# An attention layer with a second, four-token attention: next batch's token scores moved beside V on the Pool engine, the running maximum beside the V product, and the maximum spread by ScalarE

## The chip, the cores and the metric

The kernel runs on one core of one Trainium2 chip. The metric is device time in microseconds of one execution, as the median of several runs. Everything is float32. The engines that matter here are TensorE (PE in the profile), VectorE (DVE), ScalarE (ACT), GpSimd (POOL) and the DMA queue of SyncE (SP); each runs its own list of instructions in the order in which the program gives them.

## The reference

For each of 16 batches of 100 queries, ordinary attention over 718 context tokens is added to a second attention over 4 tokens, whose queries come out of a third, small attention. Shapes: x is 16x100x640, ctx is 16x722x384, eight heads of 80.

```python
enc, ca = ctx[:, :718], ctx[:, 718:]
hs = mha(x @ Wq, enc @ Wk, enc @ Wv)              # mha: softmax(q k^T / sqrt(80)) v, 8 heads
ca_q1 = einsum("btc,th->bch", ca, Wq_ca)[:, indices, :]   # indices: 100 of the 384 columns
ca_hs1 = mha(ca_q1, x, x)
ca_hs2 = mha(ca_hs1 @ Wq, ca @ Wk_ca, ca @ Wv_ca)
out = (hs + ca_hs2) @ Wout + b_out + x
```

## The kernel before

A loop over the 16 batches `b` does everything. On PE, DVE and POOL the order of instructions is the order in which the code is written (`tc.manual_schedule`); ScalarE's and the SP queue's order is made by a scheduler from the same program, and `tc.issue_after` places an instruction of ScalarE behind another one.

The 718 context tokens are cut into six chunks, worked on as three pairs (128, 128 and 103 rows each). For each pair, `scores(b, g, tiles)` multiplies keys and queries into four PSUM banks of the pool `ps4`, and ScalarE copies them into the tile `st` (L505). `larger` and L951 keep the running maximum `most` over all pairs on VectorE (two sums of SBUF tiles for a pair, written `ALU.max`).

V and the keys are formed by `Blocks`, a seven-product scheme over 2x2 blocks: `first_half` does four products into four PSUM banks and empties them into the destination (one ScalarE copy, three VectorE sums, L316 to L322), and `second_half` adds the other three into the same banks and empties them again (L327 to L333). The block sums that the scheme needs are made by POOL: `enc_sums` for each batch's context, `weight_sums` once. `values(b, i, enc)` gives V's three pairs `va`, `vb`, `vc`; `key_blocks` gives the next batch's keys `ka`, `kb`, and `last_keys` the last 128 rows of keys by plain products.

PSUM has eight banks: four of the pool `ps4` (scores, or a `room` for one `Blocks`), and four of `ps1`, taken in turn by all others: the banks of a `Blocks` without room, y, z, the transposed output, the output's product. A matmul that begins on a bank waits until whoever reads it has emptied it.

`Maximum` turns `most` into one maximum for each query: a 32x32 transposition `turned`, a reduction `quad`, four small reductions `side`, four `mx` (L547), a copy `spread` over 32 columns (L555) and a transposition back, `over`. They are steps of a generator; `top.go(n)` issues the next n. `subtract(i)` then takes `over` from pair i's scores (L930, 1600 columns), ScalarE makes the exponentials (L1066), and the product with V, `a_ps` (L1103), ends the batch on PE. VectorE divides by the sum (L1111, L1113) and adds the second attention `hs2` (L1119).

The second attention is the class `Second`: `products` (y on PE and g on VectorE), `copy` (y to SBUF by ScalarE), `scores1` (seven POOL instructions into `e1`, L624 and L631), `softmax1` (a `Maximum` of `e1` and a subtraction), `exponentials1` (ScalarE), `softmax2` (z on PE, divided by VectorE; it also issues the load of `vb` on POOL's queue, L668), `scores2`, `softmax3`, and `values2` (seven POOL instructions into `hs2`, L711 and L718). `now` is this batch's, `second` the next one's. `Last` is the output of the batch before: `load` (x by the SP queue, and POOL adds the bias), `transpose` (PE, then ScalarE into `hsT`), `project` (PE, then VectorE adds into `xn`, L787, and SP stores). Output rows are stored in tiles of 128, so `project` has 20 matmuls in most batches, none in batches 1, 5, 10 and 14, and 40 in batch 15. `keys(b + 2)` has POOL fill the matrix `m2` that `products` reads. In odd batches five products `queries` for the next two batches stand before `a_ps`.

In a middle batch PE's order before the change is: scores 0, `va` first half, scores 1, `va` second half, scores 2, transposition, `vb` and `vc` first halves, their second halves, `project`, y, z, `ka` and `kb` first halves, second halves, `last_keys`, queries (odd batches), `a_ps`. POOL's is: `values2`, `scores1` of the next batch, `keys`, then in the next batch `enc_sums`, the bias, and a wait for that batch's last subtraction.

Of the kernel before, what the change touches and what calls it, by code (L numbers as in the profile page):

```python
# [91 lines left out]
def kernel(  # L92
# [194 lines left out]
    class Blocks:  # L287
# [36 lines left out]
        def second_half(self):  # L324
            c11, c12, c21, c22 = self.to
            m = self.sum(0, ("12", "21"), ("31", "31"), last=True)
            self.copies.append(nc.scalar.copy(c11, m))  # L327
            m = self.sum(2, ("S4", "22"), ("31", "32"), last=True)
            nc.vector.tensor_tensor(c12, m, c21, ALU.add)  # L329
            m = self.sum(3, ("22", "T4"), ("32", "31"), last=True)  # L330
            nc.vector.tensor_tensor(c21, m, c21, ALU.add)
            m = self.sum(1, ("32", "32"), last=True)
            nc.vector.tensor_tensor(c22, m, c22, ALU.add)  # L333
# [12 lines left out]
    def weight_sums(to, raw):  # L346

        (w11, w12), (w21, w22) = raw
        for out, left, right, op in (
            (to[T1], w12, w11, ALU.subtract),  # L350
            (to[T2], w22, to[T1], ALU.subtract),
            (w12, w22, w12, ALU.subtract),
            (to[T4], w21, to[T2], ALU.subtract),
        ):
# [167 lines left out]
    class Maximum:  # L522


        def __init__(self, top, name):
            self.name = name
# [7 lines left out]
        def steps(self, top):  # L534
# [11 lines left out]
            for j in range(4):  # L546
                nc.vector.tensor_reduce(  # L547
                    mx[32 * j : 32 * j + 32, :],
# [6 lines left out]
            yield nc.vector.tensor_copy(spread, mx.unsqueeze(2).to_broadcast([P, NB, 32]))  # L555
# [15 lines left out]
    class Second:  # L571
# [75 lines left out]
        def softmax2(self):  # L647
# [18 lines left out]
            self.z = z  # L666
            self.vb = vb = vb_tile(f"vb_{b}")
# [239 lines left out]

    last = None
    engines = {mybir.EngineType.Pool, mybir.EngineType.PE, mybir.EngineType.DVE}
    ctx.enter_context(tc.manual_schedule(engines=engines))  # L910
    for b in range(B):
# [31 lines left out]
        if b == 0:  # L943
            now.softmax1()
        pair, copied = scores(b, 0, tiles)
        st.append(pair)
        if b == B - 1:
            now.softmax2()
        most = wide(f"most_{b}")
        top = Maximum(most, f"{b}")  # L950
# [5 lines left out]
        if b:  # L956
            va, vb, vc = (values(b, i, e_in) for i in range(NP))
            va.first_half()
        else:
            weight_sums(  # L960
                [wk2[:, j] for j in range(3)],
                [
                    [
                        wk_sb[:, c, : 4 * P].rearrange("p (i u n) -> p u i n", i=2, u=2)[:, u]
                        for u in range(2)
                    ]
                    for c in range(2)
                ],
            )
            nc.gpsimd.tensor_tensor(  # L970
                wk4, wk_sb[:, 1, 4 * P :], wk_sb[:, 0, 4 * P :], ALU.subtract
            )
            first_values(3, e_in, (act, act))
            now.exponentials1(copied)
# [7 lines left out]
        st.append(pair)  # L982
        larger(1)
# [4 lines left out]
        if b == 0:  # L988
# [6 lines left out]
        if 0 < b < B - 1:  # L995
            now.softmax1(2)
        if last:
            last.transpose()
        larger(2)
        if b == B - 2:  # L1000
            second.products()
            second.copy()
        if b == 0:
            first_values(5, e_in, (act, act), [1])
        elif b < B - 1:
            vb.first_half()
            now.softmax1(2)
            room = psum4(f"room_{b}")
            vc.first_half(room)
            now.softmax1()  # L1010
            top.go(2)
            vb.second_half()
            now.exponentials1(vb.copies[1])
            top.go(1)
            vc.second_half()
            top.go()
        else:
            vb.first_half()
            room = psum4(f"room_{b}")
            top.go(1)  # L1020
            vc.first_half(room)
            top.go(1)
            vb.second_half()
            top.go()
            subtract(0)
            vc.second_half()
            subtract(1, 2)
            last.project()


        if b + 1 < B:
            ka, kb = (key_blocks(b + 1, i, enc) for i in range(2))
            room = psum4(f"room1_{b}")
            if b:
                subtract(0)
                if last:
                    last.project()
                if b < B - 2:
                    second.products()
                now.softmax2()  # L1040
                ka.first_half(room)
                if b < B - 2:
                    with tc.issue_after(ka.copies[0].ins):
                        second.copy()
                now.scores2()
                subtract(1)
                now.softmax3()
                kb.first_half()
                less = subtract(2)
                ka.second_half()  # L1050
            else:
                second.products()
                ka.first_half(room)
                second.copy()
                kb.first_half()
                top.go()
                ka.second_half()
                subtract(0, 1, 2)
            kb.second_half()
            copies = ka.copies[1:] + kb.copies[1:] + last_keys(b + 1, enc)  # L1060
        else:
            copies = []
        for i, e in enumerate(st):
            after = copies[(0, 1, 1)[i] if b else 3] if copies else None
            with tc.issue_after(after.ins) if after else nullcontext():
                nc.scalar.activation(e, e, AF.Exp, scale=SCALE)  # L1066
        if b == B - 2:

            second.scores1()
            now.values2(less)  # L1070
            second.softmax1()
            second.exponentials1(copies[-1])
        elif 0 < b < B - 1:
            now.values2(less)
            second.scores1()
        elif b == 0:
            second.scores1()
            weight_sums(
                [wv2[:, j] for j in range(3)],
# [96 lines left out]
```

## Time and profile before

| | |
|---|---|
| median of 3 runs | 1057.51 us (1057.46 to 1057.79) |
| the profiled execution | 1057.47 us, its span 1055.8 us |
| mean granted clock of TensorE | 0.99 |
| busy: PE, DVE, POOL, ACT | 1012.4, 711.7, 505.1, 281.3 us |
| bytes moved | 59.92 MB, mean 57 GB/s |

The span runs from the first to the last instruction on the chip. A busy time is the sum of an engine's instructions; an engine can be waiting inside a stage and still have a high share over the whole. A row of the timeline gives start, duration, engine, line, operation, tiles written and read, shape, count, and in brackets the idle time before it and who ended it. A row of the waits gives who waited for whom, the total in microseconds, how often, and the longest. A row of the windows gives the busy time of each engine in a stretch and the granted clock (column PEclk).

### The profile page before, as it was taken

What the parts mean: (1) busy time and instruction counts of PE and PEld (TensorE: products, weight loads), DVE (VectorE), ACT (ScalarE), POOL (GpSimd) and SP (SyncE); (2) the same over time, 40 slices, a digit from 0 to 9 for tenths busy, and PEclk for the clock granted to TensorE, in tenths of its full rate; (3) what the DMA queues carried; (4) which work ended last, traced back from release to release, by engine and by line L of the source; (5) the groups of instructions that cost most, each with busy time, mean ns of one, the idle gap of its engine ahead of it and who ended that gap; (6) DMA issues with size and microseconds to landing.
All of it is one profiled execution on the core that took longest, in us unless ns stands there. A gap on an engine that the chain in (4) does not pass through costs nothing.

```text
span 1055.8 us, 25004 instructions
## 1 busy us (share of the span) xinstructions
PE 1012.4 (96%) x10945; PEld 745.3 (71%) x10945; DVE 711.7 (67%) x1277; ACT 281.3 (27%) x567; POOL 505.1 (48%) x439
## 2 busy tenths in 40 slices
PE   9997989999999999999999999998999999997997
PEld 6684758776686766867677676875768676685765
DVE  1348593867839686595946959377792877839884
ACT  1232221222322323223132221232222222322322
POOL 4639309056290644608365091723909047283660
PEclk9998999999999999999999999999999999999999
DMA  8631110211102020120201203011020201110100
GB/s 280 209 99 58 41 43 9 81 46 46 68 18 92 27 88 1 47 87 9 82 25 48 87 8 106 5 44 63 18 96 9 82 23 47 65 40 3 41 1 32
DMA packets 18014, 59.92 MB, mean 57 GB/s; under 512 B 2126, under 2 KB 8278, under 8 KB 14386
## 3 DMA queue, kind: packets, MB, share of 16 engines
q1 hardware_dynamic: 14658, 40.46, 11.7%
q0 software_dynamic: 2512, 16.72, 5.0%
q8 instruction: 86, 1.41, 0.6%
q10 hardware_dynamic: 736, 1.15, 0.3%
q14 instruction: 22, 0.18, 0.1%
HBM read 54.07 MB, written 4.26 MB: 55 GB/s over the span
## 4 chain that ended last, share of the span: by engine, by line
PE 63%; DVE 27%; issue 6%; ACT 3%; DMA 0%; DVEq 0%; ACTq 0%
PE a_ps L1103 11%; PE s_ps L495 11%; PE k_ps L299 9%; PE v_ps L299 8%; PE room L299 7%; PE kT_ps L437 7%; PE q_ps L412 6%; DVE mx L547 3%; DVE most L941 3%; DVE over L557 3%; ACT st L505 3%; PE v_ps L274 2%; DVE quad L539 2%; DVE turned L537 2%; DVE side L542 2%
## 5 line engine op out<-in xcount | busy, mean ns | idle before, releaser
L711 POOL TENSOR_TENSOR hs<-vb,p 100x640 f32<-100x640 f32 x64 | 82.9, 1304 | 456.4 <-DVE st L930 432.7
L299 PE MATMUL v_ps<-wv_sb,enc 128*128 128x320 f32 x480 | 154.7, 444 | 4.3 <-DVE v L320 1.7
L505 ACT COPY st<-s_ps 128x400 f32<-128x400 f32 (+1 forms) x192 | 80.5, 506 | 240.8 <-PE s_ps L495 240.6
L299 PEld LDWEIGHTS v_ps<-wv_sb,enc 128*128 128x128 f32 x480 | 85.8, 190 | 49.1 <-ACT hsT L764 8.5
L1103 PEld LDWEIGHTS a_ps<-v,st 128*64 128x64 f32 (+3 forms) x3072 | 111.1, 126 | 12.6 <-issue 12.5
L1103 PE MATMUL a_ps<-v,st 128*64 128x81 f32 (+3 forms) x3072 | 113.8, 236 | 6.3 <-DVE kT L329 6.3
L624 POOL TENSOR_TENSOR e<-ca,g 100x800 f32<-100x800 f32 x64 | 103.1, 1621 | 27.2 <-issue 21.6
L941 DVE TENSOR_TENSOR most<-most,st 128x800 f32<-128x800 f32 (+1 forms) x64 | 82.7, 1292 | 46.5 <-ACT st L505 45.4
L1111 DVE RECIPROCAL rs<-a_ps 100x4 f32<-100x4 f32 x32 | 5.8, 182 | 158.8 <-PE a_ps L1103 158.8
L495 PEld LDWEIGHTS s_ps<-qp,kT 32*128 32x128 f32 (+1 forms) x3072 | 92.3, 179 | 15.3 <-issue 7.7
L631 POOL TENSOR_TENSOR e<-e,e 100x800 f32<-100x800 f32 x48 | 99.3, 2068 | 3.8
L495 PE MATMUL s_ps<-qp,kT 32*128 32x100 f32 (+1 forms) x3072 | 100.4, 267 | 0.0
L299 PE MATMUL k_ps<-enc,wk_sb 128*128 128x359 f32 x240 | 85.0, 476 | 10.0 <-DVE xn L787 7.3
L930 DVE TENSOR_TENSOR st<-st,over 128x1600 f32<-128x1600 f32 (+1 forms) x48 | 91.5, 1910 | 0.5
L299 PE MATMUL room<-enc,wk_sb 128*128 128x359 f32 x240 | 86.2, 482 | 0.0
L299 PE MATMUL room<-wv_sb,enc 128*103 128x320 f32 x240 | 75.9, 434 | 3.1 <-DVE v L320 3.1
L718 POOL TENSOR_TENSOR hs<-hs,hs 100x640 f32<-100x640 f32 x48 | 75.8, 1579 | 3.8
L1066 ACT ACTIVATE st<-st 128x1600 f32<-128x1600 f32 (+1 forms) x48 | 72.4, 1536 | 11.0 <-DVE st L930 10.9
L299 PEld LDWEIGHTS k_ps<-enc,wk_sb 128*128 128x128 f32 x240 | 45.3, 192 | 41.5 <-DVE xn L787 13.0
L777 PE MATMUL o_ps<-wout_sb,hsT 128*128 128x320 f32 (+2 forms) x260 | 71.9, 432 | 0.0
L412 PEld LDWEIGHTS q_ps<-xT,wq_sb 128*128 128x128 f32 x400 | 67.9, 190 | 2.1 <-issue 0.5
L437 PE MATMUL kT_ps<-enc,wk_sb 128*128 128x359 f32 x210 | 68.7, 465 | 0.5 <-ACT kT L440 0.5
(133 smaller groups left out, 1578.5 us busy)
## 6 DMA issues: line engine op xcount, KB each, us to landing
enc<-in_enct SPq DMA_DIRECT2D x15, 1077.0 KB
vb<-va_d POOLq DMA_DIRECT2D x16, 1000.0 KB, 5.9
xT<-in_xt SPq DMA_DIRECT2D x8, 500.0 KB
xn<-in_x SPq DMA_DIRECT2D x11, 320.0 KB
out<-xn SPq DMA_DIRECT2D x11, 320.0 KB
ca<-in_cas SPq DMA_DIRECT2D x16, 156.2 KB
wout_sb<-in_wqt SPq DMA_DIRECT2D x1, 1600.0 KB
wq<-in_wq SPq DMA_DIRECT2D x5, 320.0 KB
```

Source lines behind the costliest of these rows:

```text
L299: nc.tensor.matmul(bank[: left.shape[1], : right.shape[1]], left, right, start=(first and i == 0), stop=(last and i == len(products) - 1), ...
L412: nc.tensor.matmul(q_ps[:, : 2 * S].rearrange("p (j s) -> p j s", j=2), wq_sb[:, c, n * P : (n + 1) * P], xT[:, :, c, :], start=(c == 0), ...
L437: nc.tensor.matmul(k_ps[:, :KH], w, a, start=(c == 0), stop=(c == CC - 1))
L495: nc.tensor.matmul(s_ps[r][:n, 256 * a + lo : 256 * a + hi], kT[rows, c, k : k + n], rhs, start=(a == 0 and c == 0), stop=(c == HC - 1), s ...
L505: copied = nc.scalar.copy(st[:, :, 2 * r * S : 2 * (r + 1) * S], s_ps[r][:n].rearrange("p (a q) -> p a q", a=2)[:, :, : 2 * S],)
L624: first = nc.gpsimd.tensor_tensor(to, self.ca[:, t, :].unsqueeze(1).to_broadcast([S, NH, S]), g[:, :, t].unsqueeze(2).to_broadcast([S, NH, ...
L631: nc.gpsimd.tensor_tensor(e, e, to, ALU.add)
L711: first = nc.gpsimd.tensor_tensor(to, vb[:S, t, :].rearrange("p (h d) -> p h d", h=NH), p2[:, :, t].unsqueeze(2).to_broadcast([S, NH, D]), ...
L718: nc.gpsimd.tensor_tensor(sums, sums, to, ALU.add)
L930: less = nc.vector.tensor_tensor(st[i], st[i], top.over[:n].unsqueeze(1).to_broadcast([n, 2, ROWS]), ALU.subtract,)
L941: nc.vector.tensor_tensor(most[:n], most[:n], st[i][:, u], ALU.max)
L1103: nc.tensor.matmul(a_v[lo:hi, h % 4], st[i // 2][:, i % 2, h * S + lo : h * S + hi], block(i, h // 4)[:, h % 4], start=(i == 0), stop=(i = ...
```

## The change

- In middle batches `now.softmax2` (z) and `second.products` and `copy` (y) come right behind the third scores, ahead of V's second and third pair; they stood behind `project`.
- `second.scores1` (the next batch's `e1`) is issued on POOL behind y, beside V; it stood behind `values2`. In batch 0 it waits for the last subtraction (`less`).
- The maximum's first steps are issued ahead of and between the first halves of `vb` and `vc`; `vb` uses the room in `ps4`, `vc` the banks of `ps1`. The first subtraction stands before `vc`'s second half.
- `Maximum` with `behind` makes two `mx` reductions in place of four, and ScalarE makes `spread` in two copies of 64 rows; `vb.second_half` puts its ScalarE copy behind them.
- `softmax1` of the next batch moves from V's stage of its own batch to the key stage of the batch before (batch 1's own stays in batch 1, behind `va`'s first half), and `exponentials1` goes behind the first ScalarE copy of `va`.
- In `second_half`, bank 1 is used and emptied second, where it was last.
- `vb`'s load is issued at the start of the batch (`now.load`).
- Batch 0: three of the four sums of Wv's blocks are made early on POOL, the fourth behind `values2`; y comes before the last plain V product; all exponentials stand behind the last key copy.
- Which ScalarE copy each exponential follows is changed: `kb`'s first, `ka`'s second, `kb`'s second.

```diff
-        def second_half(self):
+        def second_half(self, behind=None):
             m = self.sum(0, ("12", "21"), ("31", "31"), last=True)
-            self.copies.append(nc.scalar.copy(c11, m))
+            with tc.issue_after(behind.ins) if behind else nullcontext():
+                self.copies.append(nc.scalar.copy(c11, m))
+            m = self.sum(1, ("32", "32"), last=True)
+            nc.vector.tensor_tensor(c22, m, c22, ALU.add)
             m = self.sum(2, ("S4", "22"), ("31", "32"), last=True)
             nc.vector.tensor_tensor(c12, m, c21, ALU.add)
             m = self.sum(3, ("22", "T4"), ("32", "31"), last=True)
             nc.vector.tensor_tensor(c21, m, c21, ALU.add)
-            m = self.sum(1, ("32", "32"), last=True)
-            nc.vector.tensor_tensor(c22, m, c22, ALU.add)
...
     def steps(self, top):
-            for j in range(4):
+            self.scalar = scalar = self.behind is not None
+            rows = 64 if scalar else 32
+            for lo in range(0, 64 if scalar else P, 32):
                 nc.vector.tensor_reduce(
-                    mx[32 * j : 32 * j + 32, :],
+                    mx[lo : lo + 32, :],
...
-            yield nc.vector.tensor_copy(spread, mx.unsqueeze(2).to_broadcast([P, NB, 32]))
+            if scalar:
+                for lo in range(0, P, rows):
+                    with tc.issue_after(self.behind().ins):
+                        self.spreading = nc.scalar.copy(
+                            spread[lo : lo + rows],
+                            mx[:rows].unsqueeze(2).to_broadcast([rows, NB, 32]),
+                        )
+            else:
+                nc.vector.tensor_copy(spread, mx.unsqueeze(2).to_broadcast([P, NB, 32]))
+            yield
...
         if b == 0:
             now.softmax1()
+        now.load()
         pair, copied = scores(b, 0, tiles)
...
+            if b == 1:
+                now.softmax1()
...
+            weight_sums([wv2[:, j] for j in range(3)], wv_raw, range(3))
             first_values(3, e_in, (act, act))
-            now.exponentials1(copied)
...
         pair, copied = scores(b, 1, tiles)
+        if 0 < b < B - 1:
+            now.exponentials1(copied if b == 1 else va.copies[0])
         larger(1)
...
         pair, copied = scores(b, 2, tiles)
         if 0 < b < B - 1:
-            now.softmax1(2)
-        if last:
-            last.transpose()
+            now.softmax2()
         larger(2)
-        if b == 0:
-            first_values(5, e_in, (act, act), [1])
-        elif b < B - 1:
-            vb.first_half()
-            now.softmax1(2)
-            room = psum4(f"room_{b}")
-            vc.first_half(room)
-            now.softmax1()
-            top.go(2)
-            vb.second_half()
-            now.exponentials1(vb.copies[1])
-            top.go(1)
-            vc.second_half()
-            top.go()
...
+        if b == 0:
+            second.products()
+            second.copy()
+            first_values(5, e_in, (act, act), [1])
+            weight_sums([wv2[:, j] for j in range(3)], wv_raw, [3])
+            ka, kb = (key_blocks(b + 1, i, enc) for i in range(2))
+            top = Maximum(most, f"{b}", lambda: kb.copies[0])
+            top.go(1)
+            ka.first_half(psum4(f"room1_{b}"))
+            top.go(1)
+            kb.first_half()
+            top.go(1)
+            top.go()
+            less = subtract(0, 1, 2)
+            ka.second_half()
+            kb.second_half()
+        else:
+            top = Maximum(most, f"{b}", lambda: vc.copies[0])
+            if b < B - 1:
+                second.products()
+                second.copy()
+            last.transpose()
+            if b < B - 1:
+                second.scores1()
+            top.go(2)
+            vb.first_half(psum4(f"room_{b}"))
+            top.go(1)
+            vc.first_half()
+            top.go()
+            vb.second_half(top.spreading)
+            if b < B - 1:
+                now.scores2()
+            subtract(0)
+            if b == B - 1:
+                subtract(1)
+            vc.second_half()
+            if b < B - 1:
+                now.softmax3()
+                ka, kb = (key_blocks(b + 1, i, enc) for i in range(2))
+                last.project()
+                ka.first_half(psum4(f"room1_{b}"))
+                subtract(1)
+                kb.first_half()
+                less = subtract(2)
+                if b < B - 1:
+                    second.softmax1(2)
+                ka.second_half()
+                second.softmax1(1)
+                kb.second_half()
+            else:
+                subtract(2)
+                last.project()
+        if b + 1 < B:
+            copies = [kb.copies[0], ka.copies[1], kb.copies[1]]
+            final = last_keys(b + 1, enc)
...
+        if b == 0:
+            second.scores1(less)
+        elif b < B - 1:
+            now.values2(less)
+            second.softmax1()
+        if b == B - 2:
+            second.exponentials1(final[-1])
```

## The prediction

> **What bounds the kernel now.** I read the page's engine totals first, then the Tensor engine's waits, then one batch's timeline on every engine, then the granted clock around the gaps.
>
> ```profile
> PE 1012.4 (96%) x10945; PEld 745.3 (71%) x10945; DVE 711.7 (67%) x1277; ACT 281.3 (27%) x567; POOL 505.1 (48%) x439
> PE 63%; DVE 27%; issue 6%; ACT 3%; DMA 0%; DVEq 0%; ACTq 0%
> ...
> PE room L299 <- DVE v L329: 7.6, 4, 1.9
> PE k_ps L299 <- DVE xn L787: 7.3, 10, 1.0
> PE a_ps L1103 <- DVE kT L329: 6.3, 1, 6.3
> PE room L299 <- DVE v L320: 3.1, 6, 0.5
> PE k_ps L299 <- DVE z L663: 2.7, 1, 2.7
> ```
>
> PE is the bound: it is almost never idle, and nearly all its waits are for VectorE to empty a PSUM bank. So only PE's lost time can be won. I took it from PE's timeline: wherever two matmul starts lie further apart than is usual for that shape, the excess is lost. Batch by batch (0 to 15): 7.15, 4.91, 0.94, 3.47, 0.93, 6.09, 0.92, 2.09, 0.94, 2.09, 4.88, 2.09, 0.93, 2.07, 7.84, 2.50; together 49.8 us. The rest is matmul work that the change keeps, so no outcome is below about 1008. Batches 1, 5, 10 and 14 stand out: no output tile is ready there, `project` (20 matmuls, 5.4 us) is missing, and that was VectorE's time to catch up:
>
> ```profile
> 713.38 0.74 PE L652 MATMUL z_ps<-y,e 100*32 100x33 f32 x64 [0.66 <-DVE v L329]
> 716.85 2.26 PE L299 MATMUL room<-enc,wk 128*128 128x359 f32 x4 [1.93 <-DVE v L329]
> ...
> 717.40:720.70 3.30, 3.30 (x6) 1.92 (x6) 3.23 (x4) 0.00 (x0) 0.00 (x0) 0.50 0.01 4
> ```
>
> The last row is the window view (PEclk is the column with 0.50): after the gap PE runs at half clock for 3.4 us, worth 1.7 us.
>
> ```profile
> 626.19 3.46 DVE L941 TENSOR_TENSOR most<-most,st 128x800 f32<-128x800 f32 x2 [2.13 <-ACT st L505]
> 652.61 1.82 DVE L930 TENSOR_TENSOR st<-st,over 128x1600 f32<-128x1600 f32 x1
> 92.79 8.48 DVE L930 TENSOR_TENSOR st<-st,over 128x1600 f32<-128x1600 f32 x3
> 664.46 2.50 POOL L711 TENSOR_TENSOR hs<-vb,p 100x640 f32<-100x640 f32 x2 [26.79 <-DVE st L930]
> 643.93 0.87 ACT L645 ACTIVATE e<-e 100x800 f32<-100x800 f32 x1 [6.41 <-DVE e L641]
> 659.17 1.54 ACT L1066 ACTIVATE st<-st 128x1600 f32<-128x1600 f32 x1
> ```
>
> VectorE's sums of two SBUF tiles are slow while Pool works: 3.46 for two `larger` against 2.02 in batch 0, and 2.83 for a subtraction against 1.82. Its sums from PSUM are not (0.49 either way). Pool idles 26.8 us in mid-batch.
>
> **The change in a batch with project (2-4, 6-9, 11-13).** I count from the first score matmul, with starts and durations of batch 9 (616.64).
> PE: third scores end at 13.99; z 0.68, y 1.06 and the transpose 0.48 now follow (they were elsewhere, so no work is added), then V's second pair: first halves from 16.2 and 18.45, second halves 20.6 and 24.4, project 28.15 (second bank 30.84).
> VectorE: `larger(1)` now meets an idle Pool, since the next tokens' scores no longer run into this batch: 2.0 instead of 3.46. z's two operations (0.62) fit before 15.85, when ScalarE has copied the third scores. Then `larger(2)` to 17.8, g to 18.0, transposition and reduction to 19.9, V sums 21.5, side and two mx (0.74 + 0.65; two of 0.32 are dropped) 22.9, V sums 24.45.
> ScalarE spreads: a row for a copy of 64x800 is missing. Below: the exponential of 100x800, 0.87; above: that of 1600 elements, 1.54. I take 0.87, the same count of elements. Two end at 24.65, so VectorE's spread copy (0.99) is gone and `over` hardly waits, ending 25.6. Behind it in the queue stand V sums (27.0) and `scores2`'s three (0.96), so the subtraction starts at 27.96.
> Pool: g releases 12.2 us of products (four of 1.54, three of 1.88, gaps) from 18.1 to 30.3, across that subtraction. Row: 2.83 (mean of batch 0's three), ending 30.8. The next V sum frees project's second bank at 31.35 against 30.84: 0.5 lost. The Trainium skill (SBUF — State Buffer, "SBUF: two separate sides") says that the port pair is locked for a whole instruction and the loser blocks: up to 1.88 + 1.82 = 3.70, a loss of 1.4. The row is of this very instruction, so I keep 0.5; by the rule the total would be some 11 us worse.
> Key stage: softmax3 and the xn sums end at 34.7; `subtract(1)` 38.45, `subtract(2)` 41.8 with Pool idle. The next maximum's halves (1.9 and 2.1) now stand ahead of the key sums; the sum that frees last_keys' second bank ends at 47.65, wanted at 48.8: hidden by 1.1. Its spread, over and e1 (3 to 4 us) lie beside a_ps, where VectorE idled (158.8 us in front of L1111 in all). Without that cover they would hold the rs sums. The xn wait of 1.0 (ten times) goes, as three key banks no longer need it early.
> Lost: 0.5 in place of 0.92-2.09 (3.47 in batch 3): 16.5 becomes 5.0, **-11.6**.
>
> **Batches 5, 10, 14.** The V pair ends at 28.15 and keys follow at once. Key sums wait 0.1. Then VectorE, with two half maxima ahead of the sums, frees last_keys' second bank at 45.4, wanted at 43.4: a stall of 2.0, a new one in place of L329's. The clock: the gaps of 1.9 (in batches 1, 5 and 10) and 2.7 (batch 14) were each followed by half clock, those of 1.2 (batch 3) and 1.8 (batch 14) were not. The skill (TensorE: Matmul & The Clock Gate, the table of two states) throttles after an idle window of about 3.4 us, which would cost nothing here; the rows say 1.7. Mine lies at the edge, so I take half, 0.85. Sum 2.95 each: 18.8 becomes 8.9, **-9.9** (by the rule -12.5).
>
> **Batch 1** does the next maximum in its V stage (7.0 us after V's first sums); ScalarE's exponential stands in front of its copies of the third scores: z waits to 15.8 (1.8), y for a V sum 0.4. Then as above 0.3 and 2.3, clock 0.85: 5.65 for 4.91, **+0.75**.
> **Batch 0**: with `less` Pool no longer works beside the three subtractions (5.3 for 8.48) and the key sums end near 97.6, not 101.9; but the exponentials stand behind the last key copy (96.0) and end at 100.5, and PE, idle from 95.4, draws the half clock again. I take **-1.5**, between 0 and -4.
> **Batch 15**: `larger(2)` still collides with Pool's values2 (3.98), and now the transposition and reduction precede V's sums: they end about 22.9, wanted at 20.7, a stall of 2.15; project's second bank waits 1.45; 1.0 of old stalls goes: **+2.6**.
>
> **Moved and costless**: vb's DMA goes ahead of enc_sums on Pool's queue (0.58 a batch; landing 5.9 us after issue, due over 20 us later); in batch 0 it waits there for va_d, whose landing no row shows: between 0 and some 7 us (the longest vb landing), ahead of sums that PE wants only at 77.7 and which ended at 65.0. wv sums (3 x 0.86) move ahead of values2(0), which waits for p2 until 76.7: hidden. On SP the ca and enc loads stand ahead of the out stores and xn loads; the same count, and xn is due a batch later: nothing. Pool's m2 and enc_sums keep their place behind values2; without values2's early start they would reach `larger(1)` again (1.4 a batch). Swapping wk's third and fourth sum and freeing V's bank 1 first (c22 before c12) costs nothing and lets y start at 14.7, its bank being free at 12.0.
>
> Sum: -11.6 - 9.9 + 0.75 - 1.5 + 2.6 = -19.7. The profiled execution took 1057.47 (span 1055.8 and 1.67 around it), 0.04 below the median 1057.51. **1038.**
>
> **Rivals.**
> 1. *The spread decides (slower).* `over` waits in VectorE's strict order, and behind it everything to project's second bank has no slack. At 1.54 each the two copies cost 1.3 more in each of 14 batches (18), and the gaps of 1, 5, 10, 14 surely draw the clock (3.4): 1038 + 21.6 = 1060. It outweighs the gain from about 1.45 a copy. For: nothing covers it. Against: 0.87 for 800 elements. 14%.
> 2. *Pool's collision is worse.* Subtractions of 3.5 (the longest L930 here), V sums and last_keys late by 0.7 to 0.9 in 13 batches: 1048 to 1050. For: Pool's span reaches past 30; against: one subtraction of three is hit. 20%.
> 3. *The stall only moves*: the key stage's half maxima are late by 1 to 2 us in all batches too, eating the 1.1 of slack: about 1055 to 1060. 10%, split evenly over the three signs near zero.
> 4. *No clock drops, no collision*: 1028 to 1031. 10%.
> Main case 46%, its own range 1031 to 1045.
>
> **How the numbers follow.** Faster: 46 + 20 + 10 + a third of rival 3 (3) = 79, less 1 for what I overlooked: 0.78. Same (within 0.2%, 2.1 us, about what a measurement can tell): 0.05. Slower: rival 1 and the last third: 0.17. The range runs from 1026 (no collision, no clock, batch 0 at its best) to 1058, leaving out most of rival 1 and little below.
>
> **What would show it.** In the changed profile: no L941 pair above 2.1 in mid-kernel batches; ScalarE's spread rows of about 0.87; subtract(0) at 2.5 to 3 and the other two at 1.82; PE waits on o_ps for VectorE of about 0.5, on kT_ps in batches 1, 5, 10, 14 of about 2, on batch 15's V of about 2; the wait on xn gone; four half-clock stretches or fewer in the loop. I am wrong if spread rows exceed 1.4, if kT_ps waits in project batches, or if odd batches stay at 68.3.

## The result, and the profile after

The changed kernel takes 1021.03 us (median of 4 runs, 1020.68 to 1021.13), beside 1057.57 for the kernel before on the same chip: ratio 0.9654, 95% interval 0.9637 to 0.967. That is 36.5 us less, where 19.5 less was predicted; the direction was right, and the time lies below the predicted range. The profiled execution has a span of 1019.0.

The engine totals, the granted clock in 40 slices, and the shares of the chain that ended last:

```profile
PE 996.0 (98%) x10945; PEld 745.6 (73%) x10945; DVE 670.9 (66%) x1229; ACT 312.3 (31%) x599; POOL 503.5 (49%) x439
...
PEclk9999999999999999999999999999999999999999
...
PE 89%; DVE 6%; DMA 2%; SPq 1%; ACT 1%; issue 1%; DVEq 0%; ACTq 0%
```

VectorE's share of the chain fell from 27% to 6% and PE's rose from 63% to 89%: PE now almost only follows itself. VectorE lost 41 us of busy time: about 1.6 a batch for the spread copy and two mx reductions, 14 in `larger` (82.7 to 68.7), 5 in the subtractions; against these, a small subtraction of the second attention (L704) takes 0.6 instead of 0.2 in 13 batches. ScalarE gained 31, most of it the spreads (1.72 in each of the 16 batches).

PE's waits for other engines (total, how many, longest):

```profile
PE kT_ps L441 <- DVE kT L331: 5.5, 4, 1.7
PE a_ps L1110 <- DVE kT L331: 2.2, 1, 2.2
...
PE room L299 <- DVE v L318: 1.7, 1, 1.7
...
PE z_ps L668 <- ACT v L329: 1.6, 1, 1.6
...
PE o_ps L796 <- DVE v L331: 1.0, 1, 1.0
```

Each of these waits is in a batch without `project` or in batch 0 or 15. In the ten batches that have it, there is none left. (Below, a stall is the distance between two matmul starts less the usual one for that shape; it comes out about 0.15 longer than the idle time in a row's brackets. The 1.7 on kT_ps is a stall of 1.88.) That shows in project itself, in batch 9 (first score matmul at 596.62):

```profile
624.63 5.55 PE L796 MATMUL o_ps<-wout_sb,hsT 128*128 128x320 f32 x20
...
624.42 0.59 DVE L704 TENSOR_TENSOR e<-s,mx 100x32 f32<-100x32 f32 x1
624.93 1.81 DVE L959 TENSOR_TENSOR st<-st,over 128x1600 f32<-128x1600 f32 x1
626.67 0.48 DVE L331 TENSOR_TENSOR v<-v_ps,v 103x320 f32<-103x320 f32 x1
...
623.43 1.54 POOL L640 TENSOR_TENSOR e<-ca,g 100x800 f32<-100x800 f32 x1
625.04 3.45 POOL L647 TENSOR_TENSOR e<-e,e 100x800 f32<-100x800 f32 x1
...
619.51 1.72 ACT L565 COPY spread<-mx 64x800 f32<-64x800 f32 x2 [3.41 <-DVE mx L554]
```

The first row holds all 20 matmuls of project in one run without a gap. VectorE and Pool do meet, but the subtraction takes its 1.81; Pool's sum is the one held up (3.45; undisturbed 1.88). The two spread copies take 1.72, 0.86 each; 0.87 was predicted.

The batch periods (first score matmul to the next batch's first) say where the time came from:

| batches | before, us | after, us | predicted gain | measured gain |
|---|---|---|---|---|
| with project (2-4, 6-9, 11-13) | 58.6, odd ones 68.3 to 69.8 | 57.3, odd ones 65.75 | 11.6 | 21.0 |
| 5, 10, 14 | 67.25, 57.56, 60.25 | 62.36, 53.90, 53.90 | 9.9 | 14.9 |
| 1 | 66.0 | 64.57 | -0.75 | 1.4 |
| 0 | 49.46 | 47.84 | 1.5 | 1.6 |
| 15 | 57.58 | 60.02 | -2.6 | -2.4 |

The start before the loop gave another 0.3. So nearly the whole miss is in the first three lines.

### The profile page after: what moved, and what is told of

Read it like the earlier page. It is cut to its first block, busy times and chain, and to the rows that moved or that the text cites. A ratio compares the mean times of both kernels' runs of the same rounds, so it can differ in the third digit from the quotient of the medians.

```text
span 1019.0 us, 24988 instructions
## 1 busy us (share of the span) xinstructions
PE 996.0 (98%) x10945; PEld 745.6 (73%) x10945; DVE 670.9 (66%) x1229; ACT 312.3 (31%) x599; POOL 503.5 (49%) x439
## 4 chain that ended last, share of the span: by engine, by line
PE 89%; DVE 6%; DMA 2%; SPq 1%; ACT 1%; issue 1%; DVEq 0%; ACTq 0%
PE room L299 17%; PE v_ps L299 17%; PE s_ps L499 12%; PE a_ps L1110 11%; PE k_ps L299 8%; PE q_ps L416 7%; PE o_ps L796 7%; PE kT_ps L441 7%; PE y_ps L605 2%; DMA kT<-in_wkt 1%; DVE st L959 1%; PE z_ps L668 1%; SPq L207 1%; PE hst_ps L774 1%; PE v_ps L274 1%
## 5 line engine op out<-in xcount | busy, mean ns | idle before, releaser
L640 POOL TENSOR_TENSOR e<-ca,g 100x800 f32<-100x800 f32 x64 | 97.8, 1539 | 292.7 <-ACT v L316 265.1
L730 POOL TENSOR_TENSOR hs<-vb,p 100x640 f32<-100x640 f32 x64 | 82.7, 1303 | 151.9 <-DVE st L959 129.4
L299 PE MATMUL v_ps<-wv_sb,enc 128*128 128x320 f32 (+1 forms) x480 | 151.9, 439 | 0.0
L299 PEld LDWEIGHTS v_ps<-wv_sb,enc 128*128 128x128 f32 (+1 forms) x480 | 83.7, 179 | 44.6 <-issue 6.7
L647 POOL TENSOR_TENSOR e<-e,e 100x800 f32<-100x800 f32 x48 | 112.1, 2336 | 3.8
L970 DVE TENSOR_TENSOR most<-most,st 128x800 f32<-128x800 f32 (+1 forms) x64 | 68.7, 1073 | 45.4 <-ACT st L509 44.3
L959 DVE TENSOR_TENSOR st<-st,over 128x1600 f32<-128x1600 f32 (+1 forms) x48 | 86.8, 1814 | 0.0
L299 PE MATMUL room<-enc,wk_sb 128*128 128x359 f32 x240 | 82.2, 464 | 0.0
L299 PE MATMUL k_ps<-enc,wk_sb 128*128 128x359 f32 x240 | 82.2, 464 | 0.0
L299 PE MATMUL room<-wv_sb,enc 128*128 128x320 f32 x240 | 75.8, 438 | 1.7 <-DVE v L318 1.7
L441 PE MATMUL kT_ps<-enc,wk_sb 128*128 128x359 f32 x210 | 69.8, 467 | 6.0 <-DVE kT L331 5.5
L416 PE MATMUL q_ps<-xT,wq_sb 128*128 128x200 f32 x400 | 69.1, 333 | 0.0
```

The source lines that it names most:

```text
L299: nc.tensor.matmul(bank[: left.shape[1], : right.shape[1]], left, right, start=(first and i == 0), stop=(last and i == len(products) - 1), ...
L416: nc.tensor.matmul(q_ps[:, : 2 * S].rearrange("p (j s) -> p j s", j=2), wq_sb[:, c, n * P : (n + 1) * P], xT[:, :, c, :], start=(c == 0), ...
L441: nc.tensor.matmul(k_ps[:, :KH], w, a, start=(c == 0), stop=(c == CC - 1))
L640: first = nc.gpsimd.tensor_tensor(to, self.ca[:, t, :].unsqueeze(1).to_broadcast([S, NH, S]), g[:, :, t].unsqueeze(2).to_broadcast([S, NH, ...
L647: nc.gpsimd.tensor_tensor(e, e, to, ALU.add)
L730: first = nc.gpsimd.tensor_tensor(to, vb[:S, t, :].rearrange("p (h d) -> p h d", h=NH), p2[:, :, t].unsqueeze(2).to_broadcast([S, NH, D]), ...
```

## The experiments

Eleven kernels ran, each beside the kernel before on the same chip.

**1. ScalarE's spread undone in the changed kernel.**

```
- top = Maximum(most, f"{b}", lambda: vc.copies[0])
+ top = Maximum(most, f"{b}")
- vb.second_half(top.spreading)
+ vb.second_half()
```

> The changed kernel with one part undone: in batches 1 to 15 VectorE spreads the maximum itself again (four mx reductions in place of two, its own copy of 128x800), and V's second pair no longer waits for ScalarE's spread. Theory: PE's waits vanish in the batches with project because VectorE's chain from the V sums to project's second bank lost 1.6 us (0.64 for two mx and 0.97 for the spread copy), so that the first subtraction is done when PE asks for that bank. Put back, the subtraction starts near 626.5 instead of 624.93 in batch 9, behind Pool's last product sum, and the bank comes 1.5 to 2 us too late: ten batches by about 1.8, and little elsewhere, so about 1021 + 18 = 1039 (1036 to 1042), with waits on o_ps for VectorE of 1.5 to 2 us. Rival: the spread was a small part and VectorE had the time anyway (the gain comes from e1's maximum having left the V stage): 1021 to 1025, no wait on o_ps over 0.5.

Measured: 1053.99 us, ratio to before 0.9964 (0.9949 to 0.9978). Of 36.5 us only 3.8 are left (2.3 to 5.4 by the interval). Each batch with project takes 1.95 longer (59.23 and 67.69). The waits of PE, and batch 9 (which starts at 614.89 here):

```profile
PE o_ps L796 <- DVE v L331: 19.3, 11, 2.6
...
PE k_ps L299 <- DVE v L331: 4.1, 3, 1.4
...
644.18 1.06 DVE L704 TENSOR_TENSOR e<-s,mx 100x32 f32<-100x32 f32 x1
645.16 1.81 DVE L959 TENSOR_TENSOR st<-st,over 128x1600 f32<-128x1600 f32 x1
646.90 0.48 DVE L331 TENSOR_TENSOR v<-v_ps,v 103x320 f32<-103x320 f32 x1
...
643.31 1.88 POOL L647 TENSOR_TENSOR e<-e,e 100x800 f32<-100x800 f32 x1
...
642.90 2.86 PE L796 MATMUL o_ps<-wout_sb,hsT 128*128 128x320 f32 x10
647.43 2.96 PE L796 MATMUL o_ps<-wout_sb,hsT 128*128 128x320 f32 x10 [1.67 <-DVE v L331]
```

Project breaks in two. The subtraction starts 30.27 after the batch's start instead of 28.31, and 1.67 of PE's idle time follows, with a late start of the matmul behind it. The delay has two parts. The small L704 starts 1.49 later (29.29 for 27.80), which is about the two mx reductions and the copy (1.6 us); then it waits 0.47 longer for Pool's sum (1.06 for 0.59). PE loses the whole of it, 1.95 per batch: the chain from V to project has no slack. Ten batches give 19.4. Batches 5 and 10 lose 3.6 each, 14 loses 2.0 (a k_ps wait of 1.4 in each, and half clock in the first two), batch 1 loses 2.0, batch 15 loses 1.5, and 1.3 lie ahead of the loop, where this edit changes nothing. The theory's mechanism held, but it was sized only for the project batches: 1036 to 1042 was too low.

**2. The spread alone, in the kernel before** (batches 1 to 14; two mx reductions and VectorE's copy go, two ScalarE copies come; nothing else moves). In this kernel's code the two stand behind ScalarE's copy of the second half of `vc`, not of the first half as the expectation says; in batch 9 they start as soon as mx is there.

> The kernel before with one part of the change alone: in batches 1 to 14 ScalarE spreads the keys' maximum in two copies of 64x800 behind V's last first-half copy, and VectorE drops two mx reductions and its spread copy. Nothing else is moved. Theory: VectorE reaches the first subtraction about 1.5 us earlier, which takes away the waits behind it (k_ps for xn, 0.7 to 1.0 in ten batches, and some small ones) but not those of the V stage ahead of it (the room waits of 1.9 us in batches 1, 5, 10 and 14, y and z): 1057.5 - 7 to 11 = 1046 to 1051. Rival: the spread is the whole gain, as undoing it in the changed kernel cost 33 us: 1022 to 1030. Second rival: nothing, since the ends of the V stage are set elsewhere: 1056 to 1058.

Measured: 1038.03, ratio 0.9812 (0.9796 to 0.9829): 19.3 us gained, twice what I expected, though not the rival's 30. Even project batches fall from 58.6 to 57.84, odd ones to 66.5 to 67.3; these ten give 12.8 of it. In the loop, three of the four half-clock stretches of the kernel before (batches 1, 10 and 14) are gone as well, which I had not counted. With experiment 1 this makes a square of gains over the kernel before, each against its own runs on the same chip:

| | rest as before | rest changed |
|---|---|---|
| VectorE spreads | 0 | 3.8 |
| ScalarE spreads | 19.3 | 36.5 |

(It is not quite square: the second row's left kernel spreads by ScalarE in batches 1 to 14 alone, the first row's right one still does in batch 0.) Alone the spread gives 19.3 and the rest 3.8; together they give 36.5. The rest brings 17.2 only once the spread is there. The two don't add up because both work on one chain: moving e1's maximum and z takes waits away from the V stage, but without the spread VectorE reaches project's second bank too late all the same.

**3. The next tokens' scores again at the batch's end** (batches 1 to 13: Pool behind `values2`, VectorE's maximum in the next V stage).

```
-            if b == 1:
+            if b < B - 1:
                 now.softmax1()
...
-            now.exponentials1(copied if b == 1 else va.copies[0])
+            now.exponentials1(copied)
...
-            if b < B - 1:
+            if b == B - 2:
                 second.scores1()
...
-                if b < B - 1:
+                if b == B - 2:
                     second.softmax1(2)
                 ka.second_half()
-                second.softmax1(1)
+                if b == B - 2:
+                    second.softmax1(1)
...
             now.values2(less)
-            second.softmax1()
+            if b == B - 2:
+                second.softmax1()
+            else:
+                second.scores1()
```

> The changed kernel with the move of the next tokens' scores undone for batches 1 to 13: Pool computes them again behind values2, at the batch's end, and VectorE takes their whole maximum in the next batch's V stage, as the changed kernel does only in batch 1; ScalarE's spread and the early z and y stay. Theory: each of batches 2 to 13 then looks like batch 1 of the changed kernel, which loses 1.9 in front of z, 0.5 in front of y and 1.7 by half clock: 2.4 to 4.1 us each, plus a little for larger beside Pool, and less the 1.9 of the kT_ps stall in batches 5 and 10: 1021 + 30 to 45 = 1051 to 1066. Rival: ScalarE's spread was all of it, and the move of the scores is worth little: 1021 to 1030.

Measured: 1068.72, ratio 1.0107 (1.0092 to 1.0122): 1% slower than the kernel before, and a little above what I expected. Batches 2 to 13 lose 48.2 together against the changed kernel; ten half-clock stretches fall into them, where the changed kernel has none. PE's waits, and batch 9 of this kernel:

```profile
PE z_ps L668 <- ACT v L329: 36.0, 14, 5.2
...
636.84 1.54 DVE L657 TENSOR_TENSOR e<-e,over 100x800 f32<-100x800 f32 x1
638.29 2.01 DVE L970 TENSOR_TENSOR most<-most,st 128x800 f32<-128x800 f32 x2
...
638.47 0.87 ACT L661 ACTIVATE e<-e 100x800 f32<-100x800 f32 x1 [6.07 <-DVE e L657]
...
639.79 0.74 PE L668 MATMUL z_ps<-y,e 100*32 100x33 f32 x64 [2.86 <-ACT v L329]
```

The subtraction of e1's maximum ends at 638.4, and e1's exponential (638.47, 0.87) must follow; so z is late. The releaser named is ScalarE's V copy, which stands behind that exponential in ScalarE's queue. With e1's maximum in the V stage, early z and y cost more than ScalarE's spread brings: the parts of this change need one another. Early z and y, the exchanged banks of `vb` and `vc` and the earlier load of `vb` were not undone one by one.

**4. Pool idle when the first subtraction runs.** From batch 2's tokens on, Pool makes only the first of the four products of the next tokens' scores and leaves the other three and their sums out, so the second attention of this kernel is incomplete.

```
-            for t in range(T):
+            for t in range(T if b < 2 else 1):
```

> The changed kernel, but of the four products of the next tokens' scores Pool computes only the first (from batch 2's tokens on), so that Pool is idle when the first subtraction runs. Theory: VectorE pays nothing for Pool's work beside it, because its subtraction begins first and Pool's sum is the one held up (3.45 instead of 1.88 us): 1021 within 1 us, the first subtraction 1.81 as before, the small e2 sum back from 0.59 to 0.19. Rival: Pool's work beside V still costs VectorE some tenths that PE sees as small restarts: 1014 to 1018.

Measured: 1018.97, ratio 0.9634 (0.9619 to 0.9648), 2.1 less than the changed kernel. The project batches take 57.29 and 65.75, exactly as with Pool busy, so the collision costs them nothing. What is gained is 0.4 in each of batches 1, 5, 10 and 14, by the small sum:

```profile
623.21 0.19 DVE L704 TENSOR_TENSOR e<-s,mx 100x32 f32<-100x32 f32 x1
623.32 1.82 DVE L959 TENSOR_TENSOR st<-st,over 128x1600 f32<-128x1600 f32 x1
```

The 0.40 between 0.19 and 0.59 is the price of Pool's work beside V in those batches; elsewhere it disappears. I had expected 1021 within 1 and forgot the batches without project.

**5. The subtraction issued inside a Pool instruction.**

```
-            if b < B - 1:
-                now.scores2()
             subtract(0)
...
             vc.second_half()
             if b < B - 1:
+                now.scores2()
                 now.softmax3()
```

> The changed kernel with the first subtraction ahead of the three small operations of the second attention's scores (and those behind V's last sums), so that it is issued about 1.0 us earlier, at 623.6 in batch 9, inside Pool's product that runs from 623.43 to 624.97. Theory: whoever begins first keeps the SBUF path to the end of its instruction. The subtraction then waits for Pool's product and shows about 3.2 us, ending at about 626.8 as now; Pool's sum of 1.88 behind it is held up in turn. Mean of all subtractions (L959's group, its line here moved) 2.2 to 2.3 instead of 1.81; total 1020 to 1024. Rival: the two engines share in turn, so the row is 2.2 to 2.8 and the end is earlier (626.0), with the total 1019 to 1021.

Measured: 1031.67, ratio 0.9754 (0.9737 to 0.9771). Batch 9 here, and the group of all subtractions (sum and mean ns):

```profile
628.60 3.09 DVE L959 TENSOR_TENSOR st<-st,over 128x1600 f32<-128x1600 f32 x1
...
628.47 1.54 POOL L640 TENSOR_TENSOR e<-ca,g 100x800 f32<-100x800 f32 x1
630.09 3.34 POOL L647 TENSOR_TENSOR e<-e,e 100x800 f32<-100x800 f32 x1
...
L959 DVE TENSOR_TENSOR st<-st,over 128x1600 f32<-128x1600 f32 (+1 forms) x48 | 104.6, 2184 | 0.0
```

Begun 0.13 after Pool's product, the subtraction takes 3.09: it waits for the product to end (630.0) and then takes about its usual time, and now Pool's sum waits in turn. The group's sum rose by 17.8 us, 1.27 for the first subtraction of each of the 14 batches from 1 to 14. So the one that begins first keeps the path for its whole instruction, as predicted here; sharing is out. The total was missed: the project batches stay at 57.29 and 65.75, but in batches 5, 10 and 14 the kT_ps stall grows from 1.88 to 3.13 and now draws half clock. The windows around batch 14's stall (PEclk is the third column from the end), here first, and then the changed kernel's after its 1.88:

```profile
959.27 1.30 PE L441 MATMUL kT_ps<-enc,wk_sb 128*128 128x359 f32 x2 [2.96 <-DVE kT L331]
...
959.20:962.60 3.40, 3.33 (x6) 1.64 (x6) 3.23 (x6) 0.00 (x0) 3.24 (x3) 0.55 0.02 5
```

```profile
950.00:953.40 3.40, 3.35 (x44) 2.40 (x46) 3.23 (x5) 0.46 (x1) 3.24 (x3) 1.00 0.02 5
```

The same stretch holds 6 matmuls at 0.55 there and 44 at 1.00 here. Batches 5, 10 and 14 lose 2.9 each: 1.25 of stall and 1.7 of clock.

**6. The old order of the banks.** The sum of bank 1 again last in `second_half`.

> The changed kernel with V's and the keys' second halves freeing their banks in the order of before (the second bank's sum last). Theory: the order is worth nothing, since the banks rotate with it and every bank that PE asks for first is again freed by the first sum; at most y's product waits some tenths: 1020 to 1024. Rival: the order is where the 0.37 us a batch come from that no counted gap explains: 1025 to 1027, by 0.3 to 0.4 in each of fourteen batches.

Measured: 1021.56, ratio 0.9657 (0.9642 to 0.9672): no difference, and every project batch within 0.04 of the changed kernel. The order is not where the unexplained tenths come from.

**7. Key sums ahead of the half maxima where project is missing.**

```
-                if b < B - 1:
+                if last.xn:
                     second.softmax1(2)
                 ka.second_half()
-                second.softmax1(1)
+                if last.xn:
+                    second.softmax1(1)
                 kb.second_half()
```

> The changed kernel, but in the batches without project (1, 5, 10, 14) the two halves of the next tokens' maximum stand behind all key sums instead of ahead of them. Theory: those halves (2.0 and 1.9 to 2.0 us) alone make the stall of 1.88 us in front of kT_ps; moved, the bank is free in time and the chain of e1 still ends beside a_ps: 1.88 less in batches 5, 10 and 14 and 0.5 less in batch 1, 1021 - 6 = 1015 (1014 to 1016). Rival: the stall only moves, because the e1 chain now runs into the first rs and hs of a_ps, or the next batch waits for its exponential: 1018 to 1022, with a wait on a_ps or z_ps in its place.

Measured: 1013.94, ratio 0.9588 (0.9573 to 0.9602), 7.1 below the changed kernel. The three kT_ps stalls are gone (60.37, 51.91, 51.91, so 2.0 each), and batch 1 gains 0.6. The chain of e1 still ends in VectorE's idle time: nothing new shows up on a_ps or z_ps (batch 1's old wait on z_ps reads 1.9 for 1.6). The stall was a matter of order alone, with no lack of time behind it.

**8 to 11. Versions meant to beat both.** All keep experiment 7. The first also gives batch 15 its old order and starts batch 1's maximum ahead of the batch, with the exponential behind V's first copy.

> The changed kernel with its three remaining stalls taken away at once: key sums ahead of the half maxima in the batches without project (as alone in another run), batch 15 with the order of before (V's first sums ahead of transposition and reduction, second subtraction behind V's last sums), and in batch 1 the first two steps of e1's maximum ahead of the batch, in VectorE's idle time before 113.5, with the exponential behind V's first copy. Theory: 6 from the key stage, 1.8 and 1.2 less some tenths in batch 15, 1.9 to 4 in batch 1 (z's gap, y's, and the half clock if it goes with them): 1021 - 11 to -13 = 1008 to 1010. Rival: stalls are passed on to the next bank in each place, and half or less of it comes: 1014 to 1018.

Measured: 1016.52, ratio 0.9609 (0.9595 to 0.9624), worse than experiment 7 alone:

```profile
PE s_ps L499 <- ACT st L509: 2.4, 1, 2.4
...
PE o_ps L796 <- ACT v L329: 1.8, 1, 1.8
```

Both new waits are for ScalarE's queue: in batch 1 the exponential stood ahead of the copies of the second scores, in batch 15 the spread stood ahead of V's copies. The rival (the stall is passed on) was right. The second version puts the exponential back behind the copies and lets VectorE spread in batch 15:

> The second attempt at a better version. As in the first, key sums stand ahead of the half maxima in batches 1, 5, 10 and 14. New: batch 15 has the order of before whole, so VectorE spreads the maximum there (in the first attempt ScalarE's two spread copies stood in front of its copies of V's second pair, and PE waited 1.8 us for those); in batch 1 the first two steps of e1's maximum run ahead of the batch, but the exponential stays behind the copies of the second scores (in the first attempt it stood ahead of them and PE waited 2.4 us for a bank of scores). Theory: 1013.9 (key sums first alone), less 2.0 to 2.4 in batch 15, less 1.9 to 2.3 in front of z in batch 1, a little less where the half clock goes too: 1009 to 1010.5. Rival: batch 15 is bound by Pool (values2 and three xn sums beside larger) and batch 1 by ScalarE, so that no order of VectorE helps: 1013 to 1014.

Measured: 1012.44, ratio 0.9563 (0.9547 to 0.9579), better than experiment 7 but short of the 1009 to 1010.5 expected. Batch 1 falls from 64.0 to 60.36, more than expected, since half clock (PEclk 0.53 from 125.4 to 128.8 in experiment 7, 1.00 throughout here) goes with z's gap. Batch 15, which was to gain 2.0 to 2.4, rises from 60.1 to 61.5: with VectorE spreading it waits 2.8 for project's second bank (2.6 in experiment 1), and half clock follows. The third adds one line for batch 0, `final[-1 if i else -2]`, so that the first exponential goes ahead of the last key copy:

> The same, and in batch 0 the exponential of the first pair of scores goes ahead of ScalarE's last key copy, into ScalarE's idle 2.2 us there. Theory: the three exponentials end 1.3 to 1.5 us earlier, PE's gaps in front of a_ps (0.8 to 1.0 and 0.9) go, and the wait of 2.2 for the last key sum remains: 1.3 to 1.9 less than the other, 1007.5 to 1009. Rival: it delays the last key copy and the key sum's wait decides: no difference.

Measured: 1008.88 (1007.39 to 1010.95), ratio 0.9532 (0.9514 to 0.955). Batch 0 takes 45.13 instead of 47.88, more than the 1.3 to 1.9 expected: PE's gaps in front of a_ps fall by about 1.0, and the half clock there lasts 3.4 us instead of 6.8, worth 1.7. Batch 15, whose code is the same, takes 59.8 instead of 61.5 in this profile, because the same wait of 2.8 draws no half clock (see the end). The last one returns batch 15 to the changed kernel's order, but keeps its second subtraction behind V's last sums and holds Pool's values2 until `larger` is done:

> The last version with batch 15 done otherwise: the order of the changed kernel there (ScalarE spreads; transposition and reduction ahead of V's sums), but the second subtraction behind V's last sums, Pool adding the bias to the last x rows first, and Pool's values2 held until VectorE's larger is done. Batches 0, 1, 5, 10 and 14 as in the version before it, which took 1008.9; its batch 15 waits 2.9 in front of project's second bank. Theory: larger no longer runs beside Pool (4.3 and 3.6 us in the changed kernel, 2.0 alone), so V's sums come 1.6 earlier and most of the gap of 2.1 in front of V goes; the subtraction moved takes the 1.2 on o_ps away; 61.5 becomes 57 to 58 and the total 1005 to 1006. Rival: values2, held back, now runs beside the subtractions and these are what project and the last exponentials wait for: 1007 to 1009.

Measured: **1005.55** (1005.21 to 1005.72), ratio 0.9503 (0.9486 to 0.952), the best of all. `larger(2)` in batch 15, first in the changed kernel and then here:

```profile
975.63 3.64 DVE L970 TENSOR_TENSOR most<-most,st 103x800 f32<-103x800 f32 x2 [0.55 <-ACT st L509]
```

```profile
963.01 2.02 DVE L970 TENSOR_TENSOR most<-most,st 103x800 f32<-103x800 f32 x2 [2.87 <-ACT st L509]
```

Batch 15 takes 57.5 in place of 60.0, with one wait of 0.3 left on project's bank; its first subtraction takes 2.83 beside Pool, which costs less than `larger` did.

## Why the prediction was right in direction and wrong in size

*Right*: that PE waits almost only for VectorE; the spread copies (0.87 taken, 0.86 measured); `larger` at 2.0 without Pool (2.02 in batch 9); z and y without a wait; the place and size of the new stall (kT_ps, 2.0 predicted, 1.88 measured); batch 1's gap before z (1.8, measured 1.91); batch 15 (+2.6, measured +2.4, by a V stall of 1.83 and o_ps of 1.21); batch 0. The next maximum's own chain is hidden beside a_ps, as said. Rival 1, that the spread decides, named the right place with the wrong sign: at the price measured it is what the gain hangs on, and experiment 1 shows that without it 3.8 remain.

*Wrong*, 16.7 of some 17 us in four terms (of the rest, 0.3 lies ahead of the loop and as much in batches 0 and 15; and 16.5 less 5.0 is 11.5, not 11.6):

1. *The subtraction beside Pool, "Row: 2.83 ... 0.5 lost", ten times: 5.0.* It took 1.81, and nothing was lost. I took a mean of batch 0's collisions and did not ask who begins first. The rule that I set against the row has that in it: the Trainium skill (SBUF — State Buffer, "SBUF: two separate sides") gives the shared pair to whichever instruction starts first, and the other blocks. The trace agrees in both directions: VectorE first, 1.81 and Pool 3.45; Pool first, 3.09. What I drew from it, 3.70, was only the case in which Pool begins first. And the small sum ahead of the subtraction, which I left at its undisturbed length, is what waits for Pool (0.59 for 0.19) and lets the subtraction in at the very end of Pool's product. Experiment 4 removes the collision and the project batches don't move.
2. *The lost time before, "0.92-2.09": 0.33 to 0.71 too little in each project batch, 4.5 together.* Batch 8 was counted at 0.94, but its period fell by 1.27 with nothing left to count. My list took only gaps of 0.27 and more. In batch 8 of the kernel before, each of the two counted gaps (0.66 and 0.28) is followed by one more matmul start 0.10 late, and where PE passed from y to z and to the keys' first and second matmul there are three more delays of 0.10 to 0.12; after, one of 0.19 between z and y stands in place of all these. That makes 0.94 + 0.21 + 0.32 - 0.19 = 1.28; the other nine batches were not taken apart like this. Experiment 6 rules the bank order out. The floor of 1008, which was the time before less this list, falls with it: the last version takes 1005.55 with the same 10945 matmuls. A period is the safer measure: experiment 1's project batches differ by 1.95 in period where the idle time before the row reads 1.67.
3. *Batches 5, 10, 14: 5.0.* The half clock after the new stall, "so I take half, 0.85", did not come: 2.55. The stall was 0.1 shorter each and the keys' 0.1 wait did not come; the rest, about 1.8, is the undercount of term 2 again. Here the row of before misled: its gaps of 1.93 are idle time, stalls of 2.09 by the measure in which the new one was put at 2.0 and came out at 1.88. The rule of the Trainium skill (TensorE: Matmul & The Clock Gate, the table of two states), half clock after an idle window of about 3.4 us, gave the right answer for 1.88, but its edge is not the one seen here: stalls of 3.13 drew half clock three times out of three, and of those of 2.23 in experiment 1 the ones in batches 5 and 10 did (PEclk 0.55 and 0.70), those in 1 and 14 did not (1.00). The measurement decides. What separates them is how much of the stall falls into one step of a fixed grid; the last section shows it.
4. *Batch 1: 2.2.* The kT_ps stall put at 2.3 was 0.48. A likely reading, which no run isolates: z's gap and the half clock held PE up first, so that VectorE had caught up by then, and I added stalls that share one debt. Experiments 1 and 5 fit it: z's gap is the same there (1.6 of idle time), VectorE is later, and the wait on kT_ps in batch 1 is back at 2.1 and 1.9.

The two-sided bound on the collision (1.82 to 3.70) held; what failed was picking an average row, and adding losses in the range without asking whether they could all be absent. My rival 4, "No clock drops, no collision: 1028 to 1031", is what happened outside batch 1, where the half clock came behind z's gap; it still lay 7 us too high, as it kept terms 2 and 4.

## What to carry to other kernels

Find the one chain without slack and count what leaves it. 1.6 us of VectorE put back on that chain cost 1.95 us of PE per batch here, while the moves around it gave 3.8 over the whole kernel until the spread had left it. Where two engines share a path, work out which instruction begins first before pricing the collision; and when a producer has time later anyway (the half maxima, values2), put what frees a bank ahead of it. An operation handed to an idle engine stands in that engine's queue: the same spread that won 1.95 in ten batches cost 1.8 in front of V's copies in another order of batch 15.

## What the runs showed of the hardware that I had not expected

A collision of VectorE's sums of two SBUF tiles with Pool costs whichever starts second, and by the remaining length of the other: 0.13 after Pool's start, 1.28 us (3.09 for 1.81); 0.1 ahead of Pool's start, nothing. A short operation can take the wait for a long one behind it (L704: 0.19, 0.59, 1.06 by where Pool's instruction ends).

PE's half clock keeps to a fixed grid in these traces, and not to the length of a stall alone. In all 13 profiles the clock records show half-clock stretches that begin a whole number of steps of 3.413 us after the first one of the same trace and last one or two such steps (the last one of a trace can be cut short). Cut each trace into these steps, and take those that run at full clock. Where PE is idle for 2.05 us or more within one step, the next step is at half clock, 35 times of 35; where it is idle for less than 1.5, never (some 3770 steps); in between, 17 times of 40, mostly from 1.8 up. (The ends of matmuls are modelled in the profile, so these idle times are not exact.) So one and the same stall can cost clock or not. In batch 15 of the second and the third of the last four versions, whose code is the same there, PE waits 2.77 for project's second bank. In the second, 2.60 of PE's idle time falls into one step (PE busy 0.81 of 3.41), and the next runs at half clock:

```profile
980.01:983.42 3.41, 0.81 (x3) 0.65 (x4) 3.27 (x5) 1.17 (x1) 0.00 (x0) 1.00 0.00 0
983.42:986.83 3.41, 3.41 (x8) 2.06 (x8) 3.41 (x3) 1.82 (x2) 0.00 (x0) 0.50 0.00 0
```

In the third, a step ends inside the wait and splits it into 1.99 and 0.78, and the clock stays:

```profile
974.82:978.23 3.41, 1.42 (x6) 0.68 (x4) 3.34 (x3) 0.00 (x0) 0.00 (x0) 1.00 0.00 0
978.23:981.64 3.41, 2.63 (x10) 1.92 (x11) 3.31 (x6) 1.54 (x1) 0.00 (x0) 1.00 0.00 0
```

It fits the other cases. The new stall of 1.88 in batch 5 of the changed kernel is 1.73 of idle time in one step; the gaps of 1.9 before gave 1.87 to 1.93; in experiment 1 batches 5 and 10 had 2.07 and 2.06 in one step, batch 1 had 1.75, and batch 14 had 1.58 and the rest in the step before. Where the grid lies against the program differs from profile to profile, and no run tests whether a kernel can steer it. So whether a stall of 2 to 3 us costs clock was luck here. Where it did, it was dear: in experiment 5, 1.25 us more of stall cost 2.9.
